# Whole-weight loads that wait for a chosen matmul, so that they are not under way beside bunches of small tiles

## The chip, the cores and the metric

The kernel runs on one core of a Trainium2 chip, in float32. The metric is the device time of one execution in microseconds (us), as the median of the runs shown. A core has five engines with a queue each: TensorE (PE; its weight loads are shown as PEld), VectorE (DVE), ScalarE (ACT), GpSimd (POOL) and SyncE (SP), which here issues nearly all DMA transfers.

## The reference

Two layers over 32 sequences of 128 positions and 512 channels. Layer 0 is a cross attention between `x` and `ctx` over the 512 axis: norm, three 128x128 projections, a 512x512 score, softmax, weighted values, residual. Layer 1 is a gated recurrent block (RWKV style); cut to what matters:

```python
xm = xa[:, :, None] + sx[:, :, None] * (maa_stack + xxx)      # five mixes k w v r g
w = jnp.exp(-jnp.exp(time_decay + jnp.tanh(xw @ td_w1) @ td_w2))
r, k, v = xr @ Wr.T, xk @ Wk.T, xv @ Wv.T                     # 512 x 512 each
g = jax.nn.silu(xg @ Wg.T)
def step(s, rkvw):                                           # 32 heads of 16 x 16
    a = k_t[..., :, None] * v_t[..., None, :]
    out = jnp.einsum('bhi,bhij->bhj', r_t, u * a + s)
    return a + w_t[..., :, None] * s, out
x1 = x + (norm_per_head(out) * gn_w + gn_b) * g @ Wo.T
kk = jnp.square(jax.nn.relu(xk2 @ Wfk.T))
return x1 + jax.nn.sigmoid(xr2 @ Wfr.T) * (kk @ Wfv.T)
```

The initial state `s0` of each sequence is read from rows of `ctx`.

## The kernel before

**Tiles and stages.** Eight groups `g` of four sequences. A group's layer 1 has the stages front (norm, shift), mixes, gates (Wg), recurrence, head (per-head norm, Wo), norm, squares (Wfk) and rows (Wfr, Wfv, then the store). The recurrence runs twice, for channel pair `c` = 0 and 2 (two tiles of 128 channels each). It is done in doubling levels: for the block lengths 4, 8, 16, 32 a *level bunch* of small matmuls (tiles `wide`, `rk`), then the carried state (a bunch of `vp`, `t`; a bunch of `rk`, `t`), and two *output bunches* (`at`, `vp`). A bunch is 64 matmuls or so of 32x64, 64x64 or like shape, sent with no other work between them: `with K.bunch(ns)` makes them one operation for the planner. In float32 the profile shows every matmul as two records.

**Weights.** `weight(n, after)` (line 726) issues one 1 MB DMA on SP into a ring of four slots (tile `wring`). `after` is an operation that it must not precede (`K.held`). Wv stays resident (`wv`). Wfr and Wfv of a group go into the slots that Wk and Wr leave, and are not to precede the decays of channel pair 2 (`third`, line 1192). In groups 6 and 7 the feed-forward weights are loaded once for both.

**Layer 0 as filler.** `layer0(b)` (line 735) loads 256 KB of `x` and 256 KB of `ctx`; layer 0 of the next group's sequences is recorded inside the recurrence and head of this group (`ahead`, line 1056). The four pieces of `ctx` that hold a group's initial state are DMAs of 32 KB each in 64-byte runs.

**What sets the order.** Everything is recorded first, as `Op`s with the tensors that they read and write. `schedule` (line 315) then plays the program through with a cost per operation (`cost`, line 281), engine by engine, several rounds, and keeps the order with the earliest end; `order_of` (line 360) takes next the operation that can start first, with a rank to choose among those close together, and gives tiles their slots. In it a DMA takes 450 ns of SP's time, then `landing` = bytes per partition x 128 / 350 ns behind those ahead of it, with 1500 ns before and 500 after. For TensorE it also knows a limit of 280 instruction words ahead and 3200 ns to bring more (`WORDS`, `REFILL`, line 74; `late`, line 422); that a load could slow this is not in it. `words` of an operation is 4 for a matmul and 2 for a transpose. `Program.run` (line 239) sends the operations in the order kept; each engine's queue keeps that order, and the waits between engines follow from the tiles.

Of the kernel before, what the change touches and what calls it, by code (L numbers as in the profile page):

```python
# [78 lines left out]
class Tensor:  # L79


    def __init__(self, pool, shape):
        self.pool, self.shape = pool, shape
        self.slot = None
        self.writers, self.readers = [], []
        self.users = []
        self.left = 0
        pool.tensors.append(self)
# [72 lines left out]
class Op:  # L161
    __slots__ = (
        "index", "engine", "ns", "calls", "tensors", "first", "before", "after", "waits",
        "table", "end", "landing", "rank", "stage", "fed", "words", "tick", "mode", "start",
    )


class Program:
    def __init__(self, nc):
        self.nc = nc  # L170
        self.ops = []
        self.bunch_op = None
        self.stage = None
        self.held = None
        for name in OF:
            setattr(self, name, Caller(self, name))
# [33 lines left out]
    def new(self, engine):  # L210
        op = Op()
        op.index, op.engine, op.ns, op.landing = len(self.ops), engine, 0, 0
        op.calls, op.tensors, op.first = [], [], []
        op.before, op.after, op.waits, op.table, op.end = set(), [], 0, None, None
        op.fed, op.words, op.mode = set(), 0, None
        op.rank, op.stage = op.index, self.stage
        if self.held is not None:
            op.before.add(self.held)
            self.held = None
        self.ops.append(op)  # L220
        return op
# [16 lines left out]

    def run(self):
        order = schedule(self.ops)  # L240
        for op in order:
            for attr, method, args, kw in op.calls:
                f = getattr(getattr(self.nc, attr), method)
                f(*[real(x) for x in args], **{k: real(x) for k, x in kw.items()})  # L244


def real(x):
    return x.at(x.tensor.slot) if isinstance(x, View) else x
# [60 lines left out]
def shift(op):  # L309
    kind, of, sub = op.stage  # L310
    last = of >= (NG - 1) * G if kind == "first" else of >= NG - 2
    return SHIFTS.get(kind + sub, 0) + (SHIFTS.get(kind + sub + "+", 0) if last else 0)


def schedule(ops):


    for op in ops:
        for b in op.before:
            b.after.append(op)  # L320


    chain = [0.0] * len(ops)
    for op in reversed(ops):
        i = op.index
        chain[i] = op.ns + max(
            [chain[a.index] + LAG for a in op.after if a.index < i + REACH], default=0.0
        )
        op.rank = i - PULL * chain[i] + shift(op)
    best = None  # L330
    for turn in range(ROUNDS):
        order = order_of(ops)
        end = max(op.end for op in ops)
        if best is None or end < best[0]:
            best = end, order, [(t, t.slot) for op in ops for t in op.first], [op.rank for op in ops]
            since = 0
        else:
            since += 1
        if since == 4:

            for op, rank in zip(ops, best[3]):
                op.rank = rank
            since = 0
        free = 0.0
        for op in order:
            if op.engine != "PE":
                continue
            gap, free = op.start - free, op.end
            if gap < 200:
                continue  # L350
            late = op
            while late and late.end > op.start - TRACE:
                late.rank -= BLAME * min(gap, 3000) * (1 + turn % 4)
                late = max(late.before, key=lambda b: b.end, default=None)
    for t, slot in best[2]:
        t.slot = slot
    return best[1]


def order_of(ops):  # L360
# [200 lines left out]
def xattn_then_rwkv(ctx: ExitStack, tc: tile.TileContext, a: dict, out: bass.AP):  # L561
    nc = tc.nc
# [15 lines left out]
    for t in [t for p in ats for t in p.tiles] + vps.tiles:  # L578
        nc.vector.memset(t, 0.0)

    K = Program(nc)

    def bank():
        return View(Tensor(banks, [P, 512]))
# [53 lines left out]
    def constants():  # L638
        K.stage = ("constants", 0, "")

        def load(t, src):
            K.held = begun[0]
            K.sync.dma_start(t, src)

# [15 lines left out]
        for c in range(NC):  # L660
            K.tensor.transpose(
                pt[:, c * 2 * B : (c + 1) * 2 * B], rows[:, c * P : (c + 1) * P],
                ident[0 : 2 * B, 0 : 2 * B],
            )
        K.vector.tensor_copy(st.rearrange("p c r b -> p (c r b)"), pt[:, 0 : NC * 2 * B])

        def block_ones(t, pattern, first, step, width):

            K.gpsimd.memset(t, 1.0)
            K.gpsimd.affine_select(  # L670
# [674 lines left out]
```

## Time and profile before

| | |
|---|---|
| median of three runs | 1809.52 us (1807.96 to 1809.89) |
| profiled execution, its own time | 1808.94 us |
| its span, first to last instruction | 1807.2 us |
| granted TensorE clock, mean | 0.994 |
| HBM read, written | 75.93 MB, 8.39 MB |
| one whole weight, issue to landing | 5.1 to 6.6 us (medians by weight) |
| 256 KB of x or ctx, issue to landing | 2.8, 3.1 us (medians) |

A row of a group reads: engine, operation, tiles written <- tiles read, partitions x elements, count, then busy time, mean of one in ns, and the idle time of the engine before them with what ended it. In a timeline a row is a start, a duration, the engine, and how many were merged; a bracket is idle time before it. "issue" stands for idle time in which the engine waited for no other engine that the profile shows. Nearly all rows name line 244, the line of `run` that sends every operation, so tiles tell them apart. A row of stretches gives start:end, length, busy time (and count) of PE, PEld, DVE, ACT and POOL, the granted clock, the DMA share and GB/s.

### The profile page before, as it was taken

What the parts mean: (1) busy time and instruction counts of PE and PEld (TensorE: products, weight loads), DVE (VectorE), ACT (ScalarE), POOL (GpSimd) and SP (SyncE); (2) the same over time, 40 slices, a digit from 0 to 9 for tenths busy, and PEclk for the clock granted to TensorE, in tenths of its full rate; (3) what the DMA queues carried; (4) which work ended last, traced back from release to release, by engine and by line L of the source; (5) the groups of instructions that cost most, each with busy time, mean ns of one, the idle gap of its engine ahead of it and who ended that gap; (6) DMA issues with size and microseconds to landing.
All of it is one profiled execution on the core that took longest, in us unless ns stands there. A gap on an engine that the chain in (4) does not pass through costs nothing. (4 is left out here: it accounts for less than half of the span.)

```text
span 1807.2 us, 45445 instructions
## 1 busy us (share of the span) xinstructions
PE 1761.2 (97%) x20232; PEld 889.7 (49%) x20232; DVE 1170.0 (65%) x2301; ACT 706.0 (39%) x1230; POOL 310.0 (17%) x329
## 2 busy tenths in 40 slices
PE   8999999999999999999999999999999999899998
PEld 4535553455434554345543455435554445445543
DVE  9847784458835588456864568645685665786561
ACT  4424531356313553235632445324452245324321
POOL 2230015100150001600016000160001510230011
PEclk9999999999999999999999999999999999899999
DMA  6101102021020210202012020121201201001000
GB/s 204 44 24 49 37 26 87 31 64 38 24 93 24 63 38 24 93 25 75 26 47 70 25 75 26 47 71 30 76 19 55 76 25 48 3 24 50 26 13 35
DMA packets 61940, 87.23 MB, mean 48 GB/s; under 512 B 20336, under 2 KB 21488, under 8 KB 61744
## 3 DMA queue, kind: packets, MB, share of 16 engines
q1 hardware_dynamic: 61024, 84.06, 14.7%
q8 instruction: 158, 2.59, 0.6%
q10 hardware_dynamic: 720, 0.26, 0.1%
q14 instruction: 38, 0.31, 0.1%
HBM read 75.93 MB, written 8.39 MB: 47 GB/s over the span
## 5 line engine op out<-in xcount | busy, mean ns | idle before, releaser
L244 PE MATMUL bank<-t,wring 128*128 128x512 f32 x1024 | 469.0, 603 | 0.8 <-DVE t L244 0.6
L244 PE MATMUL bank<-wring,t 128*128 128x512 f32 x768 | 339.6, 595 | 0.7 <-DVE t L244 0.7
L244 PEld LDWEIGHTS bank<-t,wring 128*128 128x128 f32 x1024 | 187.2, 190 | 237.9 <-issue 204.8
L244 POOL TENSOR_TENSOR t<-t,t 128x512 f32<-128x512 f32 x192 | 239.4, 1283 | 348.8 <-DVE t L244 342.8
L244 DVE TENSOR_TENSOR t<-bank,t 128x512 f32<-128x512 f32 (+1 forms) x256 | 143.9, 586 | 224.4 <-PE bank L244 176.9
L244 POOL TENSOR_TENSOR small<-small,neg_half 128x1 f32<-128x1 f32 (+1 forms) x96 | 62.7, 660 | 1143.0 <-DVE small L244 1143.0
L244 PE MATMUL bank<-t,t 128*128 128x512 f32 x512 | 251.1, 607 | 2.2 <-ACT t L244 2.2
L244 PEld LDWEIGHTS bank<-wring,t 128*128 128x128 f32 x768 | 143.5, 190 | 185.7 <-issue 178.8
L244 ACT COPY t<-bank 128x512 f32<-128x512 f32 (+1 forms) x240 | 132.1, 588 | 229.0 <-PE bank L244 222.0
L244 ACT ACTIVATE t<-bank 128x512 f32<-128x512 f32 x120 | 71.4, 597 | 340.5 <-PE bank L244 340.4
L244 DVE SCALAR_TENSOR_TENSOR t<-bank,vec,t 128x512 f32<-128x512 f32 x192 | 131.3, 743 | 67.8 <-PE bank L244 67.8
L244 PEld LDWEIGHTS bank<-ident,t 128*128 128x128 f32 x900 | 104.6, 141 | 74.4 <-issue 42.4
L244 PE MATMUL bank<-ident,t 128*128 128x128 f32 x900 | 130.2, 276 | 3.8 <-ACT t L244 2.7
L244 ACT ACTIVATE wide<-rk,par 128x512 f32<-128x512 f32 x128 | 85.4, 715 | 123.0 <-DVE rk L244 123.0
L244 ACT ACTIVATE t<-bank,small 128x512 f32<-128x512 f32 x128 | 87.7, 690 | 106.3 <-DVE small L244 105.5
L244 PEld LDWEIGHTS bank<-t,t 128*128 128x128 f32 x512 | 87.0, 189 | 85.6 <-issue 56.3
L244 PE MATMUL bank<-t,wv 128*128 128x512 f32 x256 | 123.8, 608 | 0.0
L244 PEld LDWEIGHTS bank<-wide,rk 32*64 32x64 f32 x8192 | 95.4, 131 | 55.2 <-ACT wide L244 17.0
L244 DVE COPY_PREDICATED at<-level,bank 128x512 f32<-128x512 int32 x192 | 121.6, 705 | 0.0
L244 PE MATMUL bank<-wide,rk 32*64 32x64 f32 x8192 | 105.6, 233 | 8.3 <-issue 4.1
L244 DVE TENSOR_REDUCE small<-bank 128x1 f32<-128x512 f32 x128 | 86.0, 681 | 30.5 <-PE bank L244 30.1
L244 DVE SCALAR_TENSOR_TENSOR t<-t,vec,t 128x512 f32<-128x512 f32 x128 | 90.9, 755 | 0.1
(98 smaller groups left out, 1798.6 us busy)
## 6 DMA issues: line engine op xcount, KB each, us to landing
t<-in_ctx_dram SPq DMA_DIRECT2D x32, 256.0 KB, 3.1
t<-in_x_dram SPq DMA_DIRECT2D x32, 256.0 KB, 2.8
wring<-in_WgT_dram SPq DMA_DIRECT2D x8, 1024.0 KB, 5.1
wring<-in_WkT_dram SPq DMA_DIRECT2D x8, 1024.0 KB, 5.3
wring<-in_WrT_dram SPq DMA_DIRECT2D x8, 1024.0 KB, 5.2
wring<-in_WoT_dram SPq DMA_DIRECT2D x8, 1024.0 KB, 5.5
out_dram<-t SPq DMA_DIRECT2D x32, 256.0 KB, 2.0
wring<-in_WfkT_dram SPq DMA_DIRECT2D x7, 1024.0 KB, 5.2
```

The source lines that it names most:

```text
L244: f(*[real(x) for x in args], **{k: real(x) for k, x in kw.items()})
```

## The change

After `schedule` has kept an order, a new step `pace` goes over it. It takes the planner's starts and ends, and lists the stretches in which a *dense* TensorE operation runs (one of 64 words or more: the level, carried-state and output bunches). For every load with a landing of 500 ns or more and a reader, it looks for the first TensorE operation, ended at or after the load's planned start, behind which no dense operation runs for 2500 ns plus twice the landing. If one ends early enough (landing plus 5000 ns ahead of the first reader's start), the load waits for it: it is sent right after that operation in the common order, and a dependency on it is added by hand. The next load is looked for from that end plus one landing on. Otherwise the load stays where it was.

```diff
@@ Program.run
         order = schedule(self.ops)
+        done = {}
         for op in order:
             for attr, method, args, kw in op.calls:
                 f = getattr(getattr(self.nc, attr), method)
-                f(*[real(x) for x in args], **{k: real(x) for k, x in kw.items()})
+                done[op] = f(*[real(x) for x in args], **{k: real(x) for k, x in kw.items()})
+            if op.behind is not None:
+                self.tc.add_manual_dep(
+                    done[op].ins, done[op.behind].ins.name,
+                    mybir.DependencyInfo(
+                        mybir.DependencyClass.Sync, mybir.DependencyReason.DATA
+                    ),
+                    reason="pace",
+                )
@@ schedule
-    return best[1]
+    for op, (op.start, op.end) in zip(ops, best[4]):
+        pass
+    return pace(best[1])
+
+
+def pace(order):
+
+
+    tensor = [op for op in order if op.engine == "PE"]
+    ends = [op.end for op in tensor]
+    dense = [(op.start, op.end) for op in tensor if op.words >= 64]
+    begins = [s for s, _ in dense]
+
+    def clear(a, b):
+        i = bisect.bisect_left(begins, b) - 1
+        return i < 0 or dense[i][1] <= a
+
+    behind, at = {}, 0.0
+    for op in order:
+        if op.calls[0][1] != "dma_start" or op.landing < 500 or not op.after:
+            continue
+        latest = min(a.start for a in op.after) - op.landing - 5000
+        i = bisect.bisect_left(ends, max(op.start, at))
+        while i < len(ends) and ends[i] <= latest and not clear(ends[i], ends[i] + 2500 + 2 * op.landing):
+            i += 1
+        if i < len(ends) and ends[i] <= latest:
+            op.behind = tensor[i]
+            behind.setdefault(tensor[i], []).append(op)
+            at = ends[i] + op.landing
+    paced, met = [], set()
+    for op in order:
+        met.add(op)
+        if op.behind is None or op.behind in met:
+            paced.append(op)
+        paced += [x for x in behind.get(op, []) if x in met]
+    return paced
```

(A bracketed `@@` names the function. Left out: the new field `behind` of `Op`, the handing over of `tc`, and that `best` also keeps every operation's start and end.)

More of the change, by code (lines that the diff above doesn't have):

```diff
@@ L164, with __init__ @@
         "table", "end", "landing", "rank", "stage", "fed", "words", "tick", "mode", "start",
+        "behind",
     )
 class Program:
-    def __init__(self, nc):
-        self.nc = nc
+    def __init__(self, nc, tc):
+        self.nc, self.tc = nc, tc
         self.ops = []
@@ L215, in new @@
         op.fed, op.words, op.mode = set(), 0, None
-        op.rank, op.stage = op.index, self.stage
+        op.rank, op.stage, op.behind = op.index, self.stage, None
         if self.held is not None:
@@ L334, in schedule @@
         if best is None or end < best[0]:
-            best = end, order, [(t, t.slot) for op in ops for t in op.first], [op.rank for op in ops]
+            best = (
+                end, order, [(t, t.slot) for op in ops for t in op.first], [op.rank for op in ops],
+                [(op.start, op.end) for op in ops],
+            )
             since = 0
@@ L579, in xattn_then_rwkv @@
         nc.vector.memset(t, 0.0)
-    K = Program(nc)
+    K = Program(nc, tc)
     def bank():
```

## The prediction

> **What bounds the kernel now.** I read the page's first rows, then the waits of TensorE, the timeline of TensorE around its longest wait, the SP queue in the same stretch, and equal stretches of five groups.
>
> ```profile
> PE 1761.2 (97%) x20232; PEld 889.7 (49%) x20232; DVE 1170.0 (65%) x2301; ACT 706.0 (39%) x1230; POOL 310.0 (17%) x329
> q8 instruction: 158, 2.59, 0.6%
> ```
>
> TensorE (PE) has 46 us of idle time in a span of 1807.2 us; everything else has room. So only what stops TensorE can matter. Queue q8 is the fetch of TensorE's own program: 158 packets, 2.59 MB, that is 16 KB or 256 instructions a packet. In the waits of TensorE:
>
> ```profile
> PE bank L244 <- issue: 17.4, 20, 2.4
> PE bank L244 <- DVE t L244: 6.6, 7, 1.8
> ```
>
> 17.4 us in 20 waits end on "issue", no producer. All but a few tenths of a microsecond of it fall inside bunches of small tiles. The longest, in group 1:
>
> ```profile
> 379.23 1.02 PE L244 MATMUL bank<-t,wv 128*128 128x512 f32 x2
> 380.18 1.53 PE L244 MATMUL bank<-rk,t 32*32 32x64 f32 x95
> 384.11 1.10 PE L244 MATMUL bank<-rk,t 32*32 32x64 f32 x33 [2.39 <-issue]
> 385.14 3.17 PE L244 MATMUL bank<-t,wv 128*128 128x512 f32 x4
> 388.24 1.49 PE L244 MATMUL bank<-at,vp 64*32 64x64 f32 x128
> ```
>
> A bunch of 128 matmul records stops after 95. The SP queue at that time (start, duration of the issue):
>
> ```profile
> 376.82 0.37 SPq L244 DMA_DIRECT2D wring<-in_WfrT_dram  x1
> 379.42 0.37 SPq L244 DMA_DIRECT2D wring<-in_WfvT_dram  x1
> 379.88 0.46 SPq L244 DMA_DIRECT2D t<-in_x_dram  x1
> 380.43 5.18 SPq L244 DMA_DIRECT2D t<-in_ctx_dram  x5
> ```
>
> Two whole weights are under way (landed 382.2 and 386.3). I compared each instruction packet's start in the trace with the moment it fell due: about 140 instructions past a block's border, or the end of the packet before. Undisturbed it starts 1.0 to 1.4 us after that, 2.3 to 2.6 us when packets follow one another. The packet beside Wfr started 3.9 us after it (377.7 to 381.5), when TensorE had run 449 instructions past that border, all that it held. In groups 2 to 5 the same packet is 3.5, 3.0, 3.8 and 4.1 us late. This is the mechanism: the fetch stands behind a weight, the bunch runs dry.
>
> **What it costs.** The first four rows are groups 1 to 4 from their first bunch of small tiles to the next group's; the next five, groups 1 to 5 from the end of the last level bunch of channel pair 0 to the first one of pair 2 (start:end, length, PE busy, PEld, DVE, ACT, POOL, clock). The last is the time after the 2.39 us stop.
>
> ```profile
> 351.80:574.30 222.50, 219.22 (x2529) 110.99 (x2528) 142.88 (x285) 88.58 (x154) 37.73 (x36) 0.99 0.16 49
> 574.30:796.10 221.80, 218.00 (x2529) 110.19 (x2528) 142.82 (x285) 88.58 (x154) 37.72 (x36) 1.00 0.16 49
> 796.10:1015.60 219.50, 217.80 (x2529) 110.28 (x2528) 142.81 (x285) 88.49 (x154) 37.74 (x36) 1.00 0.16 50
> 1015.60:1237.50 221.90, 217.98 (x2529) 110.37 (x2528) 142.91 (x285) 88.67 (x154) 37.72 (x36) 1.00 0.16 49
> ...
> 371.40:404.90 33.50, 31.11 (x528) 17.18 (x526) 15.13 (x32) 16.11 (x31) 0.00 (x0) 0.95 0.29 84
> 594.00:626.90 32.90, 29.82 (x522) 16.34 (x522) 15.04 (x32) 16.05 (x31) 0.00 (x0) 1.00 0.29 86
> 815.80:846.20 30.40, 29.42 (x522) 16.30 (x522) 15.02 (x32) 15.99 (x31) 0.00 (x0) 1.00 0.31 94
> 1036.40:1068.20 31.80, 29.49 (x523) 16.27 (x522) 14.67 (x29) 15.05 (x29) 0.00 (x0) 1.00 0.29 89
> 1257.10:1289.50 32.40, 29.84 (x529) 16.52 (x526) 15.15 (x32) 16.12 (x31) 0.00 (x0) 1.00 0.29 88
> ...
> 384.00:388.00 4.00, 3.89 (x37) 2.03 (x36) 1.23 (x1) 1.33 (x2) 0.00 (x0) 0.57 0.79 191
> ```
>
> In this stretch the carried-state bunch (rk,t) takes 1.99 us and the two output bunches (at,vp) with what lies between them 4.83 us in the undisturbed pair 2. Excess over that: group 1 3.04; group 2 2.10 + 1.61; group 3 1.22; group 4 2.59; group 5 3.09. In group 1 the stop also halved the granted clock (0.57 in the last row), and the four wv matmuls took 3.17 instead of 1.98: 1.19 more. Sum 3.04 + 1.19 + 3.71 + 1.22 + 2.59 + 3.09 = **14.8 us**. Two checks: length less excess is 29.3, 29.2, 29.2, 29.2, 29.3 us, the same everywhere; and whole groups differ by just these sums (219.5 for the group with 1.2, 222.5 for that with 4.2), so a lost microsecond isn't won back later by slack on DVE or ACT. Removing it should shorten the end one for one.
>
> **The change, part by part.** `pace` looks at loads with landing of 500 ns or more in the planner's cost (1 MB: 2996, 256 KB: 749): so not weights alone, x, ctx and the larger constants too; 32 KB pieces of ctx and stores are left. I laid its rule over the trace's times.
>
> 1. Wfr, Wfv of groups 1 to 5 (10 loads). They want a stretch of 2.5 + 2 x 3.0 = 8.5 us without a dense bunch. After the release (376.8 in group 1) the first begins at 393.1, the end of the second output bunch, and reaches 404.9: Wfr goes to 393. Wfv may begin 3.0 us later, 396.1 + 8.5 = 404.6, so either there or, if no matmul ends in that sliver, after pair 2 (442.8). Both are read in the rows stage, whose stores start at 510.7: no deadline near. Gain up to 14.8.
> 2. What stays in that stretch: one x, one ctx and four pieces of ctx (380 to 388), 640 KB of 2.69 MB. After Wfv the rule's clock (`at`) stands at 399 or 446; x is read at 403.3, so its latest place is 403.3 - 5.75 = 397.5: it keeps its place. Nearest row: the third level bunch of pair 2 in group 5, which a pair x, ctx (issued 1296.3, 1297.7) stretched to 2.85 instead of 1.60 us; in groups 1 to 4 the like pair cost nothing. Bounds 0 to 7 us (half of the 14.8); I take 0.5 a group, **+2.5**, since the nearest row is 1.25 once in five and this stretch is denser.
> 3. Group 6: Wk of the next group (issued 1502.0) lies in output bunches that take 5.40 instead of 4.83: moved behind 1511.6, **-0.6**. In group 0 (160.2, 162.8) the bunches beside the loads are clean, 1.99 and 4.83: moved to 219, gain 0.
> 4. The other weights (Wg 471, Wk 500, Wr 530, Wo 535, Wfk 555 and their like) already lie clear of bunches. They wait for the first matmul that ends after their release, at most about 1 us later, with 10 us or more to their reader: 0. Their cover is that distance; without it each late microsecond would be a TensorE stop.
> 5. The waits themselves: SP waits, TensorE doesn't. SP already waits 83 times for PE, 1186.8 us in all, at no cost. Behind Wfr on SP stand Wfv and then what is emitted after 393; x (411.7, 421.4, 446.7) comes in its own place. x, ctx and the ctx pieces at 380 stand *ahead* of it now and may start a little sooner. Stores depend on nothing here.
> 6. Start and tail. In the first 30 us the DMA is the busiest resource (280 GB/s) and the constants are now spaced behind early matmuls; x of the first batches has no room and is left. Wo of group 7 (1666.7) goes behind the last bunch, 1720.2; it takes some 5.5 us and is first needed at 1731. From -2 to +4, nearest row the DVE wait of 1.14 at 12.5 us: I take **+1**.
>
> Sum: -14.8 + 2.5 - 0.6 + 1 = **-11.9**. The profiled run's span 1807.2 becomes 1795.3, its own time 1808.94 becomes 1797.0; the median of the runs shown is 0.6 above the profiled one, so **1797.6 us**.
>
> Two rules speak against this. The Trainium skill, "DMA: Bandwidth & Descriptors", section on queues, rings and completion order: each DMA engine takes turns between queues packet by packet. A weight's packets are 2 KB and take 84 ns (median in the trace between 376.8 and 382.2), so the fetch should lose a fraction of a microsecond and the change would bring next to 0; the packets here start 2.5 us later than undisturbed ones, and that decides. "Runtime: NRT & Kernel Launch", instruction fetch mechanics, gives TensorE 128 KiB of instruction memory, 2048 instructions, and calls the fetch hidden. With 2048 in store no 5 us load could starve a bunch, the sum would be 0; this trace shows the stop at 449.
>
> **Rivals.** (a) *The small loads keep the fetch late* (0.14). Item 2 at its upper end: the four ctx pieces alone are 2048 packets, and a packet of q8 behind them is as late as before. For it: the second fetch in these stretches (385.7) ran among them and was 3.2 us after its time. Against: they carry a quarter of the bytes. Gain half, 7.4 + 0.6 - 1 = 7: 1802.5.
> (b) *It doesn't do what it says* (0.08): the planner's clock puts no clear stretch where I see one, or fetches of dense bunches are slow of themselves, as in group 0 at 217.8 and group 4 at 1035.2, where 1.11 and 0.88 us are lost with no load near. 1809.5.
> (c) *Activations land late* (0.12), the one on the other side. The rule leaves x and ctx 5.75 us from the matmul's end to the reader by the planner's clock; issue to landing is 2.8 to 3.1, so 2.7 are spare. Some 28 pairs are loaded in groups 0 to 6, and each microsecond beyond the spare is a DVE wait that TensorE inherits (no slack, as the groups show). A mean lateness of 12/28 = 0.43 us eats the gain; 0.7 us gives +8: 1817. Against: in the trace they are read 12 to 16 us after issue, and most keep their place.
>
> **How the numbers follow.** The forecast has 0.66; its own range is item 2 and item 6 at their ends short of the rivals, 1793 to 1803. With (a) at 1802.5 (0.14), faster by over 0.2% (below 1805.9; 0.2% is about what a measurement of this kernel can tell) has 0.80, within 0.2% 0.08, slower 0.12. The range 1791 to 1808 leaves out (c), half of (b) and a few hundredths of a gain larger than all excess named.
>
> **What would show it.** Right: the waits of TensorE on "issue" fall from 17.4 to below 9; Wfr and Wfv are issued about 393 in group 1 and later; the stretch of the five rows takes about 29.7 us and no 0.5 clock in it. Wrong at item 2: Wfr and Wfv have moved but the bunches still stop, beside x and ctx. Wrong at 1: they still lie inside the bunches. Rival (c): new TensorE waits on DVE small or t at the start of a batch. The prediction fails outright if the groups still take 222 us without "issue" waits.

## The result, and the profile after

The changed kernel takes 1795.82 us (median of four runs, 1794.28 to 1798.06) beside 1808.74 of the kernel before: a ratio of 0.9927, 95% interval 0.9912 to 0.9942. Run again later on another chip it took 1795.59 beside 1807.55, ratio 0.9926 [0.9913, 0.9939]. The profiled execution is the slowest of the first four: 1798.06, span 1796.3 (before: 1808.94 and 1807.2). So the spans of the two profiles differ by 10.9, the medians by 12.9.

The page's engine row and the first waits of TensorE (engine, what it waited for, us in total, times, longest), after:

```profile
PE 1758.5 (98%) x20232; PEld 888.7 (49%) x20232; DVE 1171.4 (65%) x2301; ACT 706.2 (39%) x1230; POOL 310.3 (17%) x329
```

```profile
PE bank L246 <- issue: 8.2, 11, 1.4
PE bank L246 <- DVE t L246: 8.2, 7, 2.0
```

The waits that end on no producer went from 17.4 us in 20 to 8.2 in 11, the longest from 2.39 to 1.43. The other engines do what they did. TensorE in group 1, the bunches that stopped before:

```profile
382.41 1.99 PE L246 MATMUL bank<-rk,t 32*32 32x64 f32 x128
384.33 1.98 PE L246 MATMUL bank<-t,wv 128*128 128x512 f32 x4
386.24 1.48 PE L246 MATMUL bank<-at,vp 64*32 64x64 f32 x128
387.65 1.99 PE L246 MATMUL bank<-t,wv 128*128 128x512 f32 x4
389.57 1.49 PE L246 MATMUL bank<-at,vp 64*32 64x64 f32 x128
```

Each bunch runs through its 128 records, and the wv matmuls after the carried-state bunch are back at 1.98 us: no halved clock. The issues on SP in the same group show where the loads went:

```profile
391.11 0.39 SPq L246 DMA_DIRECT2D wring<-in_WoT_dram  x1
391.59 1.51 SPq L246 DMA_DIRECT2D t<-in_x_dram  x1
393.19 2.61 SPq L246 DMA_DIRECT2D t<-in_ctx_dram  x5
...
440.86 0.38 SPq L246 DMA_DIRECT2D wring<-in_WfkT_dram  x1
444.48 0.38 SPq L246 DMA_DIRECT2D wring<-in_WfrT_dram  x1
447.83 0.37 SPq L246 DMA_DIRECT2D wring<-in_WfvT_dram  x1
```

Nothing is issued beside the bunches at 379.8 to 391.1. Wo has the stretch between the two channel pairs, with x, ctx and the four pieces of ctx straight behind it; Wfk, Wfr and Wfv come after pair 2. That isn't quite what was predicted; more below. The stretches that answer to those shown of before: two whole groups, then the five stretches from the last level bunch of pair 0 to the first of pair 2 (start:end, length, busy time of PE, PEld, DVE, ACT, POOL, clock, DMA share, GB/s):

```profile
354.00:572.00 218.00, 217.56 (x2529) 110.33 (x2528) 142.79 (x285) 88.56 (x154) 37.76 (x36) 1.00 0.16 50
572.00:790.30 218.30, 217.57 (x2529) 110.16 (x2528) 142.77 (x285) 88.65 (x154) 37.76 (x36) 1.00 0.16 50
...
373.60:402.90 29.30, 29.30 (x529) 16.30 (x526) 15.17 (x32) 16.04 (x31) 0.00 (x0) 1.00 0.22 61
591.60:621.20 29.60, 29.60 (x526) 16.37 (x524) 15.12 (x32) 16.13 (x31) 0.00 (x0) 1.00 0.22 60
809.90:839.20 29.30, 29.30 (x530) 16.29 (x528) 15.17 (x32) 16.04 (x31) 0.00 (x0) 1.00 0.22 61
1029.80:1059.00 29.20, 29.20 (x523) 16.30 (x522) 14.70 (x29) 14.97 (x29) 0.00 (x0) 1.00 0.23 61
1247.80:1277.50 29.70, 29.48 (x525) 16.30 (x525) 15.08 (x32) 15.99 (x31) 0.00 (x0) 1.00 0.22 61
```

The five add up to 147.1 us, before to 161.0: 13.9 us gained where the change aims. The whole span, by the first level bunch of each group (before, after): to group 1, 351.8 and 354.0; groups 1 to 5, 1121.7 and 1109.0; groups 6 and 7, 333.7 and 333.3. So 12.7 of the 13.9 come out at the end of group 5. The missing 1.2 are a wait of TensorE on DVE near 1428 that is 2.04 instead of 0.60 long in this profile (0.58 in the second profile of the same kernel), and small leftovers. Group 0 took 212.1 instead of 210.1, as its waits on "issue" between 193 and 221 add up to 4.4 us instead of 2.7; in the second profile it took 209.1, so those 2 us are scatter of this one execution.

A closer measure of what happens to the pair 0 bunches is therefore the **sum of the five stretches**. It is used below, beside the waits on "issue" and the median. It comes from one profiled execution each, and two executions of the same kernel differ by about 1 us in it (147.1 and 148.2, 147.0 and 147.7), so smaller differences say nothing; and it does not see stops in other bunches. The medians were taken on several chips, so they are compared by their ratio to the kernel before on the same chip:

| kernel | five stretches, us | "issue", us | median, us | ratio to before [95%] |
|---|---|---|---|---|
| before | 161.0 | 17.4 | 1808.74 | |
| changed | 147.1 | 8.2 | 1795.82 | 0.9927 [0.9912, 0.9942] |
| changed, again | 148.2 | 6.5 | 1795.59 | 0.9926 [0.9913, 0.9939] |
| every load waits, bunches not avoided | 159.8 | 19.2 | 1814.27 | 1.0030 [1.0019, 1.0041] |
| small loads alone wait | 161.1 | 17.1 | 1816.39 | 1.0034 [1.0021, 1.0047] |
| Wfr, Wfv out, small loads stay | 150.7 | 8.9 | 1797.34 | 0.9930 [0.9915, 0.9945] |
| a quarter of Wfr, Wfv, earlier | 149.8 | 7.5 | 1797.17 | 0.9928 [0.9911, 0.9946] |
| a quarter of Wfr, Wfv, in place | 150.0 | 8.2 | 1797.25 | 0.9935 [0.9916, 0.9954] |
| Wfr, Wfv in four DMAs, earlier | 155.6 | 10.2 | 1800.86 | 0.9956 [0.9941, 0.9971] |
| Wfr, Wfv in four DMAs, in place | 159.2 | 15.1 | 1807.40 | 0.9983 [0.9976, 0.9990] |
| whole weights alone wait | 146.8 | 7.1 | 1793.89 | 0.9919 [0.9904, 0.9934] |
| Wfr, Wfv alone wait | 147.0 | 4.5 | 1791.85 | 0.9905 [0.9890, 0.9919] |
| the same, again | 147.7 | 7.0 | 1793.57 | 0.9921 [0.9905, 0.9937] |
| changed, REFILL 3700 | 140.1 | 2.3 | 1800.97 | 0.9962 [0.9948, 0.9976] |

(The stretch of the last row holds other work, since its order is another.)

### The profile page after: what moved, and what is told of

The parts are those of the page before. It is cut to its first block, busy times and chain, and to the rows that moved or that the text cites. A ratio compares the mean times of both kernels' runs of the same rounds, so it can differ in the third digit from the quotient of the medians.

```text
span 1796.3 us, 45435 instructions
## 1 busy us (share of the span) xinstructions
PE 1758.5 (98%) x20232; PEld 888.7 (49%) x20232; DVE 1171.4 (65%) x2301; ACT 706.2 (39%) x1230; POOL 310.3 (17%) x329
## 5 line engine op out<-in xcount | busy, mean ns | idle before, releaser
L246 ACT COPY t<-bank 128x512 f32<-128x512 f32 (+1 forms) x240 | 132.2, 589 | 218.3 <-PE bank L246 212.1
```

What stands on the lines that cost most here:

```text
L246: done[op] = f(*[real(x) for x in args], **{k: real(x) for k, x in kw.items()})
```

## The experiments

**Is it the place, or only the waiting?** The change does two things: it keeps loads off the bunches, and it holds SP, which had run ahead of the plan, to the plan. The first run keeps every wait and takes the avoidance away.

```diff
     def clear(a, b):
+        return True
         i = bisect.bisect_left(begins, b) - 1
```

> The changed kernel with the test for a clear stretch answering yes always: every load waits for the first TensorE operation that ends after its planned start, bunch or no bunch. Theory (a weight under way delays TensorE's instruction fetch, and the bunches run dry): Wo, Wfk, Wfr and Wfv of a group now all lie beside the bunches of pair 0 and 2, 4 MB in place of 2, so the waits on 'issue' rise to 20 to 35 us and the time to 1810 to 1825. Rival (what helped is that SP no longer runs ahead of the plan, wherever a load then falls): 'issue' stays near 8 us and the time near 1796.

Measured: 1814.27, "issue" 19.2. Its waits and the issues of group 1:

```profile
PE bank L246 <- issue: 19.2, 21, 2.8
```

```profile
369.09 0.39 SPq L246 DMA_DIRECT2D wring<-in_WoT_dram  x1
373.27 0.39 SPq L246 DMA_DIRECT2D wring<-in_WfkT_dram  x1
379.43 0.37 SPq L246 DMA_DIRECT2D wring<-in_WfrT_dram  x1
383.98 0.37 SPq L246 DMA_DIRECT2D wring<-in_WfvT_dram  x1
```

All four weights are issued from 369 to 384, across bunches, and the stops are back (three of them 1.9 to 2.8 us; in groups 3 and 4 the clock halves for 3.4 us after one). The longest stands in a level bunch of group 4, outside the five stretches, which is part of why their sum is only 159.8 though the kernel is slower than before. So waiting by itself brings nothing; where the loads fall does. "issue" came in just under the lower end that was expected: four weights one behind the other don't cost twice as much as two. They are issued 4 to 6 us apart and take some 5 us to land, so no more than one or two are under way at the same time, which may be the reason.

**Weights or small loads?** Two runs that part what the changed kernel moves together. In the first only Wfr and Wfv wait, for a stretch so long (16 us) that both go behind pair 2, and x, ctx and the pieces of ctx stay:

```diff
-        if op.calls[0][1] != "dma_start" or op.landing < 500 or not op.after:
+        if op.calls[0][1] != "dma_start" or op.name not in ("Wfr", "Wfv") or not op.after:
...
-        while ... and not clear(ends[i], ends[i] + 2500 + 2 * op.landing):
+        while ... and not clear(ends[i], ends[i] + 16000):
```

> Only Wfr and Wfv wait, and for a stretch of 16 us without bunches, so both go behind pair 2; x, ctx and the four 32 KB pieces of ctx of a group have no weight ahead of them any more and are free to fall beside the bunches of pair 0, 640 KB with no weight. Theory with the prediction's item 2: 'issue' 8 to 12 us, 1797 to 1801. Rival (a), the small loads alone keep the fetch late: 'issue' above 12 us, 1802 to 1806.

Measured 1797.34, "issue" 8.9. The loads beside the bunches of group 1 are now

```profile
379.80 0.34 SPq L247 DMA_DIRECT2D t<-in_x_dram  x1
380.25 3.43 SPq L247 DMA_DIRECT2D t<-in_ctx_dram  x5
...
440.86 0.38 SPq L247 DMA_DIRECT2D wring<-in_WfrT_dram  x1
444.48 0.38 SPq L247 DMA_DIRECT2D wring<-in_WfvT_dram  x1
```

The stretches add up to 150.7: the 640 KB cost 2.5 to 3.6 us over the changed kernel's two profiles (148.2, 147.1), and taking the two weights away won the other 10.3. In the whole time this can't be told: the ratio is 0.9930, that of the changed kernel 0.9927. In the second run only the small loads wait:

```diff
-        if op.calls[0][1] != "dma_start" or op.landing < 500 or not op.after:
+        if op.calls[0][1] != "dma_start" or not 500 <= op.landing < 2000 or not op.after:
```

> Only loads under 2000 ns of landing wait (x, ctx, constants); the weights run as before the change, so Wfr and Wfv stay beside the bunches of pair 0 while x and ctx leave them. Theory: the weights do the harm, 'issue' stays at 13 to 17 us, 1805 to 1809. Rival (a): most of the gain comes with the small loads, 'issue' 8 to 11 us, 1797 to 1802.

The stops stayed as expected: 161.1, "issue" 17.1. In group 1, ctx and its pieces went to 408, while one x stayed behind Wfr and Wfv at 388. But the kernel became 6.6 us slower than before on the same chip, where 1805 to 1809 had been expected. The place is the start (the issues on SP, two waits of DVE and two of TensorE, idle time in brackets):

```profile
20.49 0.42 SPq L246 DMA_DIRECT2D wring<-in_WgT_dram  x1
20.96 0.50 SPq L246 DMA_DIRECT2D wring<-in_WkT_dram  x1
21.55 0.45 SPq L246 DMA_DIRECT2D t<-in_x_dram  x1
```

```profile
30.12 0.69 DVE L246 BATCH_NORM_STATS2 small<-t 128x6 f32<-128x512 f32 x1 [2.82 <-DMA t<-in_x_dram]
34.19 0.69 DVE L246 BATCH_NORM_STATS2 small<-t 128x6 f32<-128x512 f32 x1 [2.66 <-DMA t<-in_ctx_dram]
```

```profile
35.33 0.33 PE L246 MATMUL bank<-ident,t 128*128 128x128 f32 x1 [2.29 <-DVE t L246]
37.30 2.99 PE L246 MATMUL bank<-ident,t 128*128 128x128 f32 x11 [1.64 <-DVE t L246]
```

The small loads wait for matmuls, Wg, Wk and Wr of group 0 don't, and so an x comes behind Wg and Wk on SP and its ctx behind all three. The x was issued at 21.55 and landed at 30.1, its ctx at 34.2; in the kernel before they had landed at 19.6 and 20.3. DVE and then TensorE wait, and the clock halves from 37.2 to 40.6. The first level bunch starts at 148.7 instead of 141.7: 7.0 of the 9.4 us by which this profile is longer, while groups 1 to 5 take 1121.7 us, just what they took before. This is rival (c) of the prediction, activations that land late, at one spot.

**Bytes, or a load of any size?** The kernel before with its own order, but Wfr and Wfv carry one chunk of four; three quarters of both weights are left out.

```diff
-        K.sync.dma_start(t, a[n + "T"].rearrange("(c p) o -> p c o", p=P))
+        src = a[n + "T"].rearrange("(c p) o -> p c o", p=P)
+        if n in ("Wfr", "Wfv"):
+            K.sync.dma_start(t[:, 0:1], src[:, 0:1])
+            K.ops[-1].landing = NC * E * 4 * P / 350
+        else:
+            K.sync.dma_start(t, src)
```

> The kernel before the change, its order and its places of the loads kept, but Wfr and Wfv carry a quarter of their bytes (256 KB each; three quarters of both weights are left out, the matmuls read what lies in the slot). Theory: what matters is how long a load is under way; each takes some 2.8 us in place of 5.2, so half to all of the 14.8 us goes: 'issue' 8 to 12 us, 1796 to 1802. Rival: any load in flight delays a fetch by the same 2.5 us, whatever its size: 'issue' 14 us or more, 1804 to 1809.

1797.17, as the theory said ("issue" 7.5 was even below its range), but with a flaw: chunk 0 of the slot is released earlier by the matmuls, so Wfr was issued at 369.0 instead of 376.8, ahead of the bunches. The run was repeated with the last chunk, `t[:, NC - 1 : NC]`:

> As the run in which Wfr and Wfv carry a quarter of their bytes (three quarters of both are left out), but the quarter is now the last of the four chunks, which the matmuls release last, so that Wfr and Wfv are issued where they are before the change (beside the carried-state and output bunches), not some 8 us earlier. Theory (the delay of a fetch goes with the bytes in flight): 'issue' 8 to 12 us and 1796 to 1802, as there. If instead the earlier place was what helped there: 'issue' above 13 us, 1803 to 1808.

The issues on SP in group 1, and then TensorE there:

```profile
376.60 0.34 SPq L244 DMA_DIRECT2D wring<-in_WfrT_dram  x1
379.20 0.34 SPq L244 DMA_DIRECT2D wring<-in_WfvT_dram  x1
```

```profile
379.95 1.99 PE L244 MATMUL bank<-rk,t 32*32 32x64 f32 x128
381.87 1.98 PE L244 MATMUL bank<-t,wv 128*128 128x512 f32 x4
383.79 1.14 PE L244 MATMUL bank<-at,vp 64*32 64x64 f32 x92
385.17 0.62 PE L244 MATMUL bank<-at,vp 64*32 64x64 f32 x36 [0.24 <-issue]
```

Now the loads are issued where they were before the change, and the bunch that stopped for 2.39 us runs through; what is left is 0.24. 1797.25 and 150.0: with three quarters of the bytes gone, 11.0 of the 13.9 us go, although two weight loads and all the small ones are still there. What counts is how much is in flight, or how long, which comes to the same here.

**Would smaller DMAs let the fetch in?** The same 2 MB in place, as four DMAs of 256 KB for each weight:

```diff
+        if n in ("Wfr", "Wfv"):
+            with K.bunch(450):
+                for c in range(NC):
+                    K.sync.dma_start(t[:, c : c + 1], src[:, c : c + 1])
+            K.ops[-1].landing = NC * E * 4 * P / 350
```

> The kernel before the change with its order and plan, but each Wfr and Wfv is sent as four DMAs of 256 KB back to back, the same bytes at the same place. If a fetch waits until all that the queue has taken is through (theory: the packets of instructions start when the load beside them lands), nothing is gained: 'issue' 14 to 19 us, 1806 to 1812. If it waits only for the one DMA under way, or takes turns between DMAs, the delay falls to a quarter: 'issue' 8 to 11 us, 1796 to 1801.

1800.86 with "issue" 10.2: this lies in the range that was to speak for the split (1796 to 1801). But it has the same flaw: the chunks of Wfr went out one by one as the slot was released, from 367.1 on. With the last chunk first (`for c in reversed(range(NC))`) all of them wait for the full release:

> As the run with four DMAs of 256 KB in place of each Wfr and Wfv, but the last chunk first, so that all four wait for the full release and 2 MB go where they went before the change. Theory (a fetch waits until what the queue has taken is through): no gain, 'issue' 14 to 19 us, 1805 to 1811. If the split itself lets a fetch in between: 'issue' 8 to 11 us, 1796 to 1801.

The same two views:

```profile
377.83 1.77 SPq L244 DMA_DIRECT2D wring<-in_WfrT_dram  x4
380.43 2.65 SPq L244 DMA_DIRECT2D wring<-in_WfvT_dram  x4
```

```profile
383.05 0.74 PE L244 MATMUL bank<-rk,t 32*32 32x64 f32 x35 [0.33 <-issue]
383.72 1.98 PE L244 MATMUL bank<-t,wv 128*128 128x512 f32 x4
385.64 1.10 PE L244 MATMUL bank<-at,vp 64*32 64x64 f32 x89
388.42 0.64 PE L244 MATMUL bank<-at,vp 64*32 64x64 f32 x39 [1.68 <-issue]
```

1807.40 and 159.2: 1.8 of the 13.9 us, and a ratio of 0.9983, a small gain that is clear of 1. In group 1 the stop moves from one bunch to the next and stays. So cutting a load up opens hardly a gap for the fetch. Since the same four DMAs with an earlier start gave 1800.86, most of the gain of the first form goes with its earlier start.

**Which waits are needed?** First only the whole weights wait, then only Wfr and Wfv, by the change's own rule:

```diff
-        if op.calls[0][1] != "dma_start" or op.landing < 500 or not op.after:
+        if op.calls[0][1] != "dma_start" or op.landing < 2000 or not op.after:
```

```diff
-        if op.calls[0][1] != "dma_start" or op.landing < 500 or not op.after:
+        if op.calls[0][1] != "dma_start" or op.name not in ("Wfr", "Wfv") or not op.after:
```

> The changed kernel, but only loads of 2000 ns of landing or more wait (the 1 MB weights); x, ctx and the constants are left as they were. Theory: the weights are all that matters, 1794 to 1798, 'issue' 7 to 10 us; the start, where the constants' waits cost some tenths, is no slower. Rival: the waits of x and ctx carry part of the gain, 1799 to 1803.

> The changed kernel, but only Wfr and Wfv wait; Wfr takes the stretch between the pairs with x, ctx and its pieces behind it on SP, Wfv goes behind pair 2; Wo and Wfk run ahead as before the change. Theory: these two weights hold the whole gain, 1794 to 1798. Rival (pinning Wo and Wfk to the plan is part of it): 1799 or more.

1793.89 and 1791.85: the first a hair under the expected range, the second 2 us under it, and both under the rival's 1799. With Wo not waiting, Wfr takes the stretch between the pairs, and the small loads stand behind it:

```profile
387.09 0.37 SPq L247 DMA_DIRECT2D wring<-in_WfrT_dram  x1
387.55 1.19 SPq L247 DMA_DIRECT2D t<-in_x_dram  x1
388.83 2.59 SPq L247 DMA_DIRECT2D t<-in_ctx_dram  x5
```

Waits for two weights of seven are enough for the whole gain. As the second looked 4 us better than the changed kernel, both were run on one chip:

> The kernel in which only Wfr and Wfv wait, again, on one chip with the changed kernel. If the 4 us that it was ahead are real (its first dense bunch at 140.2 and group 0 at 209.5 us, against 141.9 and 212.1 in the changed kernel's profile): 1790 to 1793 and 2 to 5 us under the changed kernel. If they were scatter of the fetch in group 0 and of the chip: within 2 us of it.

> The changed kernel itself, for the comparison on one chip: 1794 to 1798.

1793.57 and 1795.59: 2 us apart with intervals that overlap by most of their width, at the border of the two expectations. The version with waits for Wfr and Wfv alone is at least as fast as the changed kernel; that it is faster isn't shown.

**What of the rest?** 8.2 us on "issue" were left. The planner was told a slower fetch:

```diff
-WORDS, REFILL = 280, 3200
+WORDS, REFILL = 280, 3700
```

> The changed kernel with REFILL 3700 in place of 3200 in the planner, near the spacing of 3.5 to 3.8 us that instruction packets showed when one followed another. The planner then sets bunches further apart and finds another order. Theory: what is left of 'issue' (8.2 us) is bunches that come faster than the fetch, and falls to 3 to 6 us; the time 1790 to 1797, if the new order costs nothing elsewhere. Rival: the leftover is scatter of the fetch and the new order moves more than it brings: 1797 to 1806.

TensorE's waits:

```profile
PE bank L246 <- DVE t L246: 14.1, 11, 2.6
...
PE bank L246 <- issue: 2.3, 4, 0.7
```

"issue" fell to 2.3, lower than expected, which fits the theory that the leftover is bunches that come faster than instructions do. The traces have the rates: a bunch of 128 matmul records with its 128 weight loads uses up one packet of 256 instructions in 1.5 to 2.0 us, and in none of them do two packets start less than 3.2 us apart. But the new order has 14.1 us of waits on DVE in place of 8.2, which takes back all that "issue" lost, and the whole takes 1800.97: the rival's case.

## Why the prediction was right, and where it was not

Predicted 1797.6 (range 1791 to 1808), measured 1795.82; the case of faster by over 0.2%, given 0.80, came true.

- **The price of the stops** (14.8 us) held. The changed kernel's stretches are 13.9 us shorter, and are 29.2 to 29.7 long where 29.2 to 29.3 had been worked out as undisturbed and 29.7 was forecast. In the second profile they are 12.8 shorter, with one of 30.5. That nothing is won back later held too: groups 1 to 5 became 12.7 us shorter. (The check on whole groups fits group 4 only roughly, 2.4 us longer than group 3 where the sums give 1.4; its stop of 0.88 us at 1035.2 lies outside them.)
- **The mechanism** held in each direction: weights out of the bunches, gain; waits without avoidance, none; fewer bytes in place, gain; only the small loads out, none. How the fetch comes to stand behind the loads stays open.
- **Where the loads go** (item 1, and item 4 for Wo and Wfk) was wrong. Wfr was to go to 393 and stayed out until 444.5; Wo and Wfk were to move by 1 us and moved by 79 and 108 (312.3 to 391.1, 332.5 to 440.9). I had laid the rule over the *trace's* issue times. The rule reads the *planner's*. There `K.held` keeps Wo behind the decays of pair 2, and with the waits but without the avoidance Wo goes out at 369.1; in the program that was sent before no such wait exists, and its trace has Wo at 312.3, ahead of the group's first bunch at 351.8. The time didn't suffer: Wo lands at 396.3 and isn't needed before the head, after 440.8.
- **What stays** (item 2, +2.5) followed from the same mistake. Wo, at the head of SP's queue, has the small loads behind it, also in the run in which they have no waits of their own, so nothing stays and the term is 0 here. Its size was not far off: with the small loads left beside the bunches the stretches are 2.5 to 3.6 longer.
- **Group 6** (item 3, -0.6): Wk did move behind the output bunches, which now end at 1501.1, with Wo at 1501.2 and Wk at 1504.3. But with no load beside them they still take 5.26 instead of 5.40: gain 0.14. The term compared them with the 4.83 of pair 2 in group 1, where other work lies between the two bunches (two matmul records of 128x512 and eight of 128x128 there, four of each in group 6).
- **Start** (item 6, +1): 142.0 instead of 141.7 to the first bunch in this profile, 140.1 in the second: nothing that can be told from scatter. The danger named in rival (c) is real, as the run with small loads alone shows at 7 us; in the changed kernel Wg, Wk and Wr wait too (22.4 to 29.3 instead of 17.0 to 18.1), so that the x comes ahead of them.
- **The two rules** weighed there fare differently. The second, a store of 2048 instructions, would have made the stops impossible, and they are there, at 449. The first was read too narrowly. The Trainium skill, "DMA: Bandwidth & Descriptors", section on queues, rings and completion order, counts about 9 to 17 descriptors to a packet, 64 at most. The trace's 84 ns belong to one piece of 2 KB. If such a piece is one descriptor, an estimate from that page's figures and the 84 ns is 0.8 to 1.4 us a turn, at most 5.4. The delays of 3.0 to 4.1 us, against some 1.2 undisturbed, don't refute taking turns of that size; no run here tells the size of a turn.

So the main term is right by its mechanism, and the closeness of the total is in part luck. The forecast change was -11.9; the spans of the two profiles give -10.9 and the medians -12.9. In the profiles the sum is -13.9 in the stretches, +1.2 lost elsewhere in groups 1 to 5, +2.0 in group 0, +0.3 at the start and -0.4 in groups 6 and 7, which is the -10.9 up to rounding. Of the forecast's small terms, 2.5 for loads that did not stay, -0.6 for group 6 and 1 for the start, none came out as forecast, and scatter between executions is as large as they are.

## What to carry to other kernels

Look at waits of TensorE that end on no producer, and at what the DMA queues carry beside them: where many small matmuls run one behind the other, as in the bunches here, a megabyte or two in flight can keep the instructions from coming in time and stop the engine. Move such loads to stretches of large matmuls, which use instructions slowly (in the kernel before, 52 matmul records in the 11 us from 394 to 405, against 128 in 2 us of a bunch), or carry fewer bytes there; cutting them up in place brought little here. When you work out where a rule will put something, use the times that the rule reads, and ask whether an order in a planner is a wait in the program at all.

## What the runs showed of the hardware that was not expected

The fetch's delay grows with the bytes in flight; the number of DMAs that they are sent in matters less. The table gives, from the packets of the trace, how long after it fell due the packet for the first and the second stop of each group started (groups 1, 2, 3, 4, 5; "due" as in the prediction, a reckoning that fits bunches: in stretches of large matmuls it gives over 5 us with no load near, as at 1062.8 in the kernel before).

| kernel | first packet, us late | second packet |
|---|---|---|
| before, 2 MB of weights | 3.9, 3.5, 3.0, 3.8, 4.1 | 3.2, 3.4, 4.0, 2.6, 2.5 |
| four DMAs each, in place | 2.2, 2.6, 2.7, 2.7, 3.0 | 3.9, 3.7, 3.7, 2.7, 2.9 |
| a quarter of the bytes, in place | 1.3, 1.7, 1.2, 2.2, 2.5 | 2.0, 2.3, 2.2, 2.0, 2.4 |
| small loads alone beside the bunches (Wfr, Wfv out) | 1.1, 1.7, 1.3, 1.5, 2.1 | 2.0, 2.0, 2.1, 1.1, 2.1 |
| changed, no load | 0.9, 1.2, 1.1, 1.1, 1.4 | 1.3, 1.3, 1.2, 1.1, 1.7 |

The first column is the clearer one. In the second, the packets of the kernel before follow straight on the one ahead of them, and such packets start 2.3 to 2.6 us after its end even undisturbed; its 2.6 and 2.5 are therefore no delay. The split makes the first packet less late and leaves the second about as late as it was.

Before the change the first packet starts 0.7, 0.7 and 1.0 us ahead of the landing of Wfr in groups 1 to 3 (381.5 and 382.2, 603.9 and 604.6, 825.4 and 826.4), as if it had stood behind nearly all of that load. In groups 4 and 5 it starts 2.1 and 2.7 us after that landing, with Wfv under way (1049.1 after 1047.0, 1270.4 after 1267.7). So it isn't simply the end of the first load that lets it through, and which resource makes it stand there no run tells.

The other point is small: a stop can cost a second time. After the one of 2.39 us in group 1 the clock was halved for the next 3.4 us; stops of 1.9 to 2.4 us in groups 2, 4 and 5 were not followed by that, nor was one of 2.80 in the run without avoidance, while one of 1.95 there was. So the length alone does not decide it.
